# The count behind the last jump moved to the end of VectorE's work, and the transfers of a skipped loop given to GpSimd

## The chip, the cores and the metric

The kernel runs on one core of one Trainium2 chip. A core has five engines, each with an instruction stream of its own: TensorE (PE in the profile, its weight loads PEld), VectorE (DVE), ScalarE (ACT), GpSimd (POOL) and SyncE (SP), which here issues nearly all transfers. The engines wait for each other through semaphores. Sixteen DMA engines move the data. The metric is the time of one execution on the device in microseconds (us); lower is better.

## The reference

One transformer layer on 8,192 tokens (4 sequences of 2,048) of width 256, in float32: an attention inside chunks of 32 tokens without a softmax, a layer norm, a gated feed-forward part with integer weights, a second layer norm.

```python
Q, K, V = x @ W_q.T, x @ W_k.T, x @ W_v.T
decay = sigmoid(log_decay[0])
mask = where(diff >= 0, decay ** diff, 0)              # inside a chunk of 32
S = einsum('bncd,bnkd->bnck', Qc, Kc) * mask
O = einsum('bnck,bnkd->bncd', S, Vc)
a = sigmoid(x @ W_g.T) * O @ W_o.T + x
x = layernorm(x + a)
gate, up = x @ (w_gate / 127).T, x @ (w_up / 127).T    # 768 hidden features
x = layernorm(x + (silu(gate) * up) @ (w_down / 127).T)
```

The feed-forward weights are int32. `setup_inputs` draws them from -127 to 127.

## The kernel before, in words

The 8,192 tokens are taken in 16 blocks of 512 (`TB`). The Python loop `for b in range(NB - 2)` (line 938) is unrolled into one long program. Each pass runs the feed-forward part of block b while it prepares the attention of the blocks after it, so that TensorE always has products to do. A planner places the instructions of each engine; where the order matters it is pinned: `in_turn` (line 290) keeps an instruction behind all that were written before it for the same engine. Passes are alike and take 31.69 us each.

The feed-forward products split each float32 operand into a high and a low part, and this is exact enough only while every integer weight is at most 128 in magnitude (`EXACT`). So the kernel looks at the weights. `look_up` (line 264) takes the largest magnitude of each of nine weight pieces on VectorE, and `count_wide` (line 276), called in the pass b = 1 (line 978), counts how many of those maxima are above 128: a comparison, a product with ones on TensorE that adds over the partitions, a sum on VectorE into `count`, and a conversion to the integer `n_wide`.

After the last block's store comes the part for wide weights (lines 1174 to 1196). `nc.values_load` reads `n_wide` into a register of each of the five engines, and `tc.If(wide_any > 0)` makes each engine jump over the part if the count is 0, which it is with these inputs. The part itself holds nine transfers of weight pieces with a scaling of each, and a loop on the chip, `tc.For_i`, over all blocks; its body is `wide_block` (line 1128), which loads xT and x, computes the layer anew and stores. None of it is executed here, but it stands in the instruction streams, and what follows the jump has to bring the semaphores to what they would be had the part been run.

The transfers of the unrolled passes and of the skipped part are written with the same helpers: `load_xT` (116), `load_xn` (124) and `store` (857), which take a `start` that is `None` in the passes and the loop's register in the skipped part. All of them issue on SyncE's queue. The last block is finished group by group (lines 1102 to 1125): four groups of 128 tokens, of which ScalarE scales the first two and VectorE the last two (`by_vector`, line 874); each is stored by a transfer of its own of 128 KB (`store_groups`, line 1034, whose transfer is line 1037). What closes the program (semaphore waits and an exchange of all engines) is shown at line 1235.

Of the kernel before, what the change touches and what calls it, by code (L numbers as in the profile page):

```python
# [50 lines left out]
I32 = mybir.dt.int32  # L51
# [3 lines left out]
P = 128  # L55
# [16 lines left out]
def kernel(  # L72
# [15 lines left out]
    nc = tc.nc  # L88
# [7 lines left out]
    const = ctx.enter_context(tc.tile_pool(name="const", bufs=1))  # L96
# [12 lines left out]
    def bank(name):  # L109
        return psum.tile([P, TB], F32, tag="ps", name=name)  # L110


    def span(b, start):
        return slice(b * TB, (b + 1) * TB) if start is None else bass.ds(start, TB)

    def load_xT(b, start=None, pieces=1):
        xt = xin.tile([P, KD, TB], F32, tag="xT", name=f"xT_{b}")
        src = xT[:, span(b, start)].rearrange("(k p) t -> p k t", p=P)
        n = KD // pieces
        for k in range(0, KD, n):  # L120
            nc.sync.dma_start(xt[:, k : k + n, :], src[:, k : k + n, :])
        return xt

    def load_xn(b, start=None):
        xn = xin.tile([P, NG, D], F32, tag="x", name=f"x_{b}")
        nc.sync.dma_start(xn, x[span(b, start), :].rearrange("(g p) d -> p g d", p=P))
        return xn

    def load_w(eng, w, name):
# [146 lines left out]
    def count_wide():  # L276

        wide = const.tile([P, top.shape[1]], F32, tag="wide", name="wide")
        nc.vector.tensor_scalar(wide, top, EXACT, None, ALU.is_gt)
        ones = const.tile([P, 1], F32, tag="ones", name="ones")  # L280
        nc.vector.memset(ones, 1.0)
        pw = bank("pw")
        nc.tensor.matmul(pw[:1, : top.shape[1]], lhsT=ones, rhs=wide, start=True, stop=True)
        count = const.tile([1, 1], F32, tag="count", name="count")
        nc.vector.tensor_reduce(count, pw[:1, : top.shape[1]], mybir.AxisListType.X, ALU.add)
        n_wide = const.tile([1, 1], I32, tag="n_wide", name="n_wide")
        nc.vector.tensor_copy(n_wide, count)
        return n_wide

    def in_turn(ins):  # L290
        tc.keep_in_program_order(ins)
# [57 lines left out]
    def root_in_turn(mv, kind, name):  # L349
        return root(mv, name, kind[0], order=in_turn)  # L350
# [45 lines left out]
    def normalize(r, scale, shift, groups=range(NG)):  # L396
        for g in groups:
            in_turn(
                nc.scalar.activation(  # L399
                    r[:, g, :],  # L400
                    r[:, g, :],
                    AF.Identity,
                    bias=shift[:, g : g + 1],
                    scale=scale[:, g : g + 1],
                )
            )
# [319 lines left out]
    def move_h(b, h):  # L726

        sq = moved.tile([P, D // SQ, NG, SQ], F32, tag="sq", name=f"sq_{b}")
        for g in range(NG):
            in_turn(
                nc.vector.transpose(
                    sq[:, :, g, :], h[:, g, :].rearrange("p (j f) -> p j f", f=SQ)
                )
            )
        hT = moved.tile([P, KD, NQ, NG * SQ], F32, tag="hT", name=f"hT_{b}")
        for q in range(NQ):
            for j in range(NQ):  # L740
                nc.sync.dma_start(
                    hT[j * SQ : (j + 1) * SQ, :, q, :],
                    sq[q * SQ : (q + 1) * SQ, j::NQ, :, :].rearrange(
                        "p k g t -> p k (g t)"
                    ),
                )
        return hT
# [107 lines left out]
        return r, mv, made  # L855

    def store(b, r, start=None):
        nc.sync.dma_start(
            out[span(b, start), :].rearrange("(g p) d -> p g d", p=P), r
        )  # L860

# [76 lines left out]
    for b in range(NB - 2):  # L938
        n = b + 2
        m = b + 3  # L940
        more = m < NB
        xns[n] = load_xn(n)
        hT = hTs.pop(b)
        uT = [], []
        yT, v, sg = ahead
        steady = b > 0
        if b:
            normalize(hs[b + 1], *scales_h)
            moving = move_h(b + 1, hs[b + 1])
        ffn_up(b, hT, uT, range(0, 1))  # L950
        if b == 0:
            g_rest()
            x_sums = token_sums(xTs[m], f"x_{m}")
        ffn_up(b, hT, uT, range(1, 2))
        sT = attn_scores(n, yT)
        if m + 1 < NB:
            xTs[m + 1] = load_xT(m + 1)
        ffn_up(b, hT, uT, range(2, 3))
        if b == 0:

            normalize(hs[b + 1], *scales_h)
            moving = move_h(b + 1, hs[b + 1])
        if not more:
            normalize(r_before, *scales_out)
            store(b - 2, r_before)
        if more:
            v_next, v_rest = split_v(m, x_sums)
        multiply = ffn_up(b, hT, uT, range(3, 4), held=True)
        if more:
            v_rest()  # L970
        multiply()
        goT = attn_values(n, sT, v, sg)
        if scales_out is not None and more:
            normalize(r_before, *scales_out)
            store(b - 2, r_before)
        if b == 0:
            look_up(range(4, n_pieces))
        if b == 1:
            n_wide = count_wide()
        if more:  # L980
            go_sums = token_sums(goT, f"go_{n}")
            y_next, y_rest = split_y(m, x_sums)
        ffn_up(b, hT, uT, range(4, KH))
        r_before = r_out
        if more:
            y_rest()
            sg_next, g_rest = split_gate(m, x_sums)
            hs[n], out_rest = split_out(n, go_sums)
            g_rest()
            mv_h = out_rest()  # L990
            ahead = y_next, v_next, sg_next
            hTs[b + 1] = split_h(b + 1, moving)
            std_h = root_in_turn(mv_h, of_h, f"h_{b}")
            if b:
                mv_before, std_before = mv_out, root_in_turn(mv_out, of_out, f"out_{b}")
            back_to_sigmoids()
            if m + 1 < NB:

                x_sums = token_sums(xTs[m + 1], f"x_{m + 1}", in_turn)

            def between():
                return scale_and_shift(mv_h, std_h, of_h, f"h_{b}")

            r_out, mv_out, scales_h = ffn_down(b, uT, hs.pop(b), between)
            if b:
                scales_out = scale_and_shift(mv_before, std_before, of_out, f"out_{b}")
        else:

            hs[n] = attn_residual(n, goT)
            mv_h = moments(hs[n], f"a{n}", order=in_turn)  # L1010
            std_out = root_in_turn(mv_out, of_out, f"out_{b}")
            hTs[b + 1] = split_h(b + 1, moving)
            std_h = root_in_turn(mv_h, of_h, f"h_{b}")
            back_to_sigmoids()
            scales_out = scale_and_shift(mv_out, std_out, of_out, f"out_{b}")
            normalize(r_before, *scales_out)
            store(b - 1, r_before)

            inverse(std_h, slice(0, NG), HALF)
            for g in range(NG):  # L1020
                by_vector(hs[n], g, mv_h, std_h)
            r_out, mv_out, _ = ffn_down(b, uT, hs.pop(b), chunkwise=True)
            scales_out = iterated_scale_and_shift(mv_out, of_out, f"out_{b + 1}")
# [104 lines left out]
    def wide_block(start, weights):  # L1128
# [42 lines left out]
        project_back("w", (uT,), (rows,), residual, "fdn")  # L1171
        finish("w", r, start)

    wide_any = nc.values_load(
        n_wide, min_val=0, max_val=top.shape[1] * P, skip_runtime_bounds_check_because="a count"
    )
    with tc.If(wide_any > 0):

        homes = [
            pool.tile([P, KD, TB], F32, tag=tag, name=f"wide_{i}")  # L1180
            for i, (pool, tag) in enumerate(
                ((work, "hT_hi"), (work, "hT_hi"), (sums, "x_sums"), (sums, "g_sums"))
            )
        ]
        last_home = work.tile([P, TB], F32, tag="hT_lo", name="wide_last")
        room = [t[:, k, :] for t in homes for k in range(KD)] + [last_home]
        weights = []
        for w in (ffn_gT, ffn_uT, ffn_dT):
            weights.append([])
            for src in int_pieces(w):  # L1190
                t = room.pop(0).rearrange("p (k n) -> p k n", n=D)
                nc.sync.dma_start(t.bitcast(I32), src)
                nc.vector.tensor_scalar(t, t.bitcast(I32), SCALE, None, ALU.mult)
                weights[-1].append(t)
        with tc.For_i(0, NT, TB) as start:
            wide_block(start, weights)
# [42 lines left out]
```

## Time and profile before

| | us |
|---|---|
| median of 3 runs | 528.29 (527.94 to 528.46) |
| the profiled execution | 527.63 |
| its span, first to last instruction | 525.9 |
| outside its span | 1.73 |

| engine | busy us | share of the span |
|---|---|---|
| TensorE | 517.3 | 98% |
| VectorE | 389.8 | 74% |
| GpSimd | 343.2 | 65% |
| ScalarE | 322.3 | 61% |

The end of the program in this execution, in us from the span's start:

| what | when |
|---|---|
| TensorE reads the count, jumps | 517.2, 517.8 (the jump takes 2.245) |
| GpSimd reads the count | 519.2 |
| ScalarE reads the count | 520.2 |
| last scaling on VectorE | 520.80 to 521.21 |
| VectorE reads the count | 520.8 |
| last store issued on SyncE | 521.24, held 1.41 |
| SyncE reads the count, jumps | 522.7, 523.3 |
| SyncE's semaphore instructions behind the jump | 523.5 to 524.5 |
| closing waits and exchange | 524.5 to 525.8 |

Times come from the hardware profiler, which records one execution. An engine's name with a q behind it (SPq, PEldq) stands for the instructions of its sequencer: register loads, branches, semaphores, and the issuing of transfers; these are not counted as busy. A line number is one of the kernel before. DMA queues are numbered: 1 is SyncE's transfers, 8 and 14 bring instructions.

### The profile page before, as it was taken

The page shows a single profiled execution, that of the slowest core. Times are in us where ns is not written, and L with a number is a line of the kernel's source. Part 1 is how long each engine was busy: PE and PEld are TensorE (multiplying, and loading weights), DVE is VectorE, ACT ScalarE, POOL GpSimd, SP SyncE. Part 2 cuts the span into 40 slices and gives each one's busy share as a digit, 9 for nine tenths or more (in the row PEclk, how much of TensorE's full clock was granted, in tenths as well). Part 3 has the DMA queues.
Part 4 walks back from the last instruction along what each step waited for, and adds up shares of the span by engine and source line. Part 5 has one row for each costly group of instructions (what it writes and reads, how often), then busy time and mean ns, then how long its engine had stood idle before and what let it go on. Part 6 is the DMA issues. An engine that isn't in the chain of part 4 may idle for free.

```text
span 525.9 us, 10552 instructions
## 1 busy us (share of the span) xinstructions
PE 517.3 (98%) x3646; PEld 422.2 (80%) x3646; DVE 389.8 (74%) x964; ACT 322.3 (61%) x644; POOL 343.2 (65%) x476
## 2 busy tenths in 40 slices
PE   8999999999999999999999999999999999999994
PEld 5798887887978788887887978788887888878683
DVE  3878797686786867777677776867868677787865
ACT  2745565465656756666575655666666575667744
POOL 6535785766847668585776857668485675735653
PEclk9999999999999999999999999999999999999998
DMA  7721121213213131131312313141131312011201
GB/s 252 218 91 42 51 60 28 65 42 67 96 34 87 53 110 41 39 109 31 105 42 51 112 30 92 49 113 41 36 93 51 105 42 53 30 27 54 79 22 65
DMA packets 43256, 36.90 MB, mean 70 GB/s; under 512 B 4800, under 2 KB 39104, under 8 KB 43200
## 3 DMA queue, kind: packets, MB, share of 16 engines
q1 hardware_dynamic: 42240, 35.41, 23.2%
q8 instruction: 30, 0.49, 0.4%
q10 hardware_dynamic: 960, 0.79, 0.4%
q14 instruction: 26, 0.21, 0.2%
HBM read 20.45 MB, written 8.39 MB: 55 GB/s over the span
## 4 chain that ended last, share of the span: by engine, by line
PE 95%; DVE 2%; ACT 1%; POOL 1%; issue 0%; DVEq 0%; ACTq 0%
PE fg L776 16%; PE fu L776 16%; PE fdn L663 14%; PE p_v L462 9%; PE p_y L444 9%; PE p_g L444 9%; PE p_o L462 8%; PE po L637 5%; PE ps L616 3%; PE fdn L842 2%; PE pa L663 1%; PE pg L558 1%; PE pi L178 1%; PE pv L596 1%; PE py L575 1%; DVE st_f L311 0%
## 5 line engine op out<-in xcount | busy, mean ns | idle before, releaser
L801 POOL TENSOR_TENSOR u_lo<-u,u_hi 128x512 f16<-128x512 f32 (+1 forms) x98 | 123.0, 1257 | 111.0 <-ACT u_hi L800 109.6
L800 ACT CAST u_hi<-u 128x512 fp32r<-128x512 f32 (+1 forms) x98 | 59.7, 609 | 65.3 <-DVE u L798 64.9
L786 DVE SCALAR_TENSOR_TENSOR s<-fg,s 128x512 f32<-128x512 f32 (+1 forms) x98 | 65.9, 673 | 34.3 <-ACT s L784 34.1
L784 ACT ACTIVATE s<-fg 128x512 f32<-128x512 f32 (+1 forms) x98 | 56.9, 583 | 41.5 <-PE fg L776 41.4
L798 DVE TENSOR_TENSOR u<-fu,s 128x512 f32<-128x512 f32 (+1 forms) x98 | 66.4, 678 | 10.4 <-POOL u_lo L801 1.1
L776 PE MATMUL fg<-hT_hi,fg_hi 128*128 128x512 f32 (+1 forms) x196 | 74.0, 458 | 0.0
L776 PE MATMUL fu<-hT_hi,fu_hi 128*128 128x512 f32 (+1 forms) x196 | 60.5, 390 | 0.0
L776 PE MATMUL fg<-hT_lo,fg_lo 128*128 128x512 f16 (+1 forms) x196 | 58.0, 377 | 0.0
L776 PE MATMUL fu<-hT_lo,fu_lo 128*128 128x512 f16 (+1 forms) x196 | 57.4, 375 | 0.0
L663 PE MATMUL fdn<-fd_hi,u_hi 128*128 128x256 f32 x312 | 46.9, 292 | 0.0
L776 PEld LDWEIGHTS fu<-hT_hi,fu_hi 128*128 128x128 f32 x196 | 36.5, 188 | 8.5
L399 ACT ACTIVATE h<-h,shift_h,scale_h 128x256 f32<-128x256 f32 x52 | 27.0, 590 | 24.1 <-POOL shift_h L362 24.1
L776 PEld LDWEIGHTS fg<-hT_hi,fg_hi 128*128 128x128 f32 x196 | 34.6, 189 | 8.8
L663 PEld LDWEIGHTS fdn<-fd_hi,u_hi 128*128 128x128 f32 x312 | 39.8, 189 | 0.3
L663 PE MATMUL fdn<-fd_lo,u_lo 128*128 128x256 f16 x312 | 38.6, 273 | 0.0
L776 PEld LDWEIGHTS <-fu_lo 128*128 128x128 f16 x196 | 19.2, 98 | 22.2
L824 DVE SCALAR_TENSOR_TENSOR r<-fdn,h 128x512 f32<-128x512 f32 x30 | 20.7, 689 | 21.6 <-PE fdn L663 19.1
L759 POOL TENSOR_TENSOR hT_lo<-hT,hT_hi 128x512 f16<-128x512 f32 x28 | 35.3, 1280 | 1.2 <-ACT hT_hi L758 1.2
L776 PEld LDWEIGHTS <-fg_lo 128*128 128x128 f16 x196 | 15.3, 98 | 20.7 <-issue 12.9
L663 PEld LDWEIGHTS <-u_lo 128*128 128x128 f16 x312 | 28.4, 98 | 4.2
L462 PE MATMUL p_v<-v_sums,x_sums 128*128 128x128 f32 x240 | 31.7, 275 | 0.0
L637 PE MATMUL po<-sT,v 128*128 128x128 f32 x256 | 31.2, 275 | 0.0
(207 smaller groups left out, 1183.0 us busy)
## 6 DMA issues: line engine op xcount, KB each, us to landing
x<-in_x_dram SPq DMA_DIRECT2D x16, 512.0 KB, 3.5
xT<-in_xT_dram SPq DMA_DIRECT2D x15, 512.0 KB, 4.3
hT<-sq SPq DMA_DIRECT2D x224, 32.0 KB, 1.9
out_dram<-r SPq DMA_DIRECT2D x14, 512.0 KB, 5.0
fg_int<-in_ffn_gT_dram SPq DMA_DIRECT2D x3, 256.0 KB, 7.8
fu_int<-in_ffn_uT_dram SPq DMA_DIRECT2D x3, 256.0 KB, 7.0
fd_int<-in_ffn_dT_dram SPq DMA_DIRECT2D x3, 256.0 KB, 5.9
xT<-in_xT_dram SPq DMA_DIRECT2D x2, 256.0 KB, 4.2
```

What stands on the lines that cost most here:

```text
L399: nc.scalar.activation(r[:, g, :], r[:, g, :], AF.Identity, bias=shift[:, g : g + 1], scale=scale[:, g : g + 1],)
L444: nc.tensor.matmul(pb, lhsT=a[i - 1], rhs=b[i - 1], start=first, stop=True, skip_group_check=True,)
L462: nc.tensor.matmul(pb[:, g * P : (g + 1) * P], lhsT=b[i - 1][:, g * P : (g + 1) * P], rhs=a[i - 1], start=first and g == 0, stop=True, ski ...
L637: nc.tensor.matmul(po[:, cols], lhsT=v[:, g, dc * P : (dc + 1) * P], rhs=sT[:, cols], start=True, stop=True,)
L663: nc.tensor.matmul(pb[:, j * D : (j + 1) * D], lhsT=part[:, g * P : (g + 1) * P], rhs=w, start=(i == 0), stop=(i == len(terms) - 1),)
L759: nc.gpsimd.tensor_tensor(in_order[1], whole, in_order[0].bitcast(F32), ALU.subtract)
L776: nc.tensor.matmul(pb, lhsT=w[kind][:, dc, hc * P : (hc + 1) * P], rhs=hT[kind][:, dc, cols], start=(kind == kinds[0] and dc == 0), stop=( ...
L784: order(nc.scalar.activation(s, pg, AF.Sigmoid, scale=SCALE / H_UP))
L786: gated = nc.vector.scalar_tensor_tensor(s, pg, U_UP / H_UP**2, s, ALU.mult, ALU.mult)
L798: in_steady_turn(nc.vector.tensor_tensor(u, pu, s, ALU.mult))
L800: nc.scalar.copy(hi, u)
L801: nc.gpsimd.tensor_tensor(lo, u, hi.bitcast(F32), ALU.subtract)
```

## The change

Three things are changed.

The conversion of the count to an integer leaves `count_wide`, which now returns the float `count`. It is written just ahead of `nc.values_load`, pinned with `in_turn` behind everything that VectorE did before.

`load_xT`, `load_xn` and `store` choose their queue by `start`: SyncE in the unrolled passes as before, GpSimd in the loop of the skipped part.

The nine transfers of weight pieces in the skipped part are issued by GpSimd instead of SyncE. With this, nothing in the skipped part is issued by SyncE.

```diff
+    def queue(start):
+
+        return nc.sync if start is None else nc.gpsimd
+
     def load_xT(b, start=None, pieces=1):
...
-            nc.sync.dma_start(xt[:, k : k + n, :], src[:, k : k + n, :])
+            queue(start).dma_start(xt[:, k : k + n, :], src[:, k : k + n, :])
...
     def load_xn(b, start=None):
         xn = xin.tile([P, NG, D], F32, tag="x", name=f"x_{b}")
-        nc.sync.dma_start(xn, x[span(b, start), :].rearrange("(g p) d -> p g d", p=P))
+        src = x[span(b, start), :].rearrange("(g p) d -> p g d", p=P)
+        queue(start).dma_start(xn, src)
         return xn
...
         nc.vector.tensor_reduce(count, pw[:1, : top.shape[1]], mybir.AxisListType.X, ALU.add)
-        n_wide = const.tile([1, 1], I32, tag="n_wide", name="n_wide")
-        nc.vector.tensor_copy(n_wide, count)
-        return n_wide
+        return count
...
     def store(b, r, start=None):
-        nc.sync.dma_start(
+        queue(start).dma_start(
             out[span(b, start), :].rearrange("(g p) d -> p g d", p=P), r
         )
...
         if b == 1:
-            n_wide = count_wide()
+            count = count_wide()
...
+
+    n_wide = const.tile([1, 1], I32, tag="n_wide", name="n_wide")
+    in_turn(nc.vector.tensor_copy(n_wide, count))
     wide_any = nc.values_load(
         n_wide, min_val=0, max_val=top.shape[1] * P, skip_runtime_bounds_check_because="a count"
     )
...
-                nc.sync.dma_start(t.bitcast(I32), src)
+                nc.gpsimd.dma_start(t.bitcast(I32), src)
```

## The prediction

> **What bounds the kernel now.** I read the page from the top, then the chain, then the last stage engine by engine, because the changed lines act only at block 1 and after the last store.
>
> ```profile
> span 525.9 us, 10552 instructions
> PE 517.3 (98%) x3646; PEld 422.2 (80%) x3646; DVE 389.8 (74%) x964; ACT 322.3 (61%) x644; POOL 343.2 (65%) x476
> ...
> PE 95%; DVE 2%; ACT 1%; POOL 1%; issue 0%; DVEq 0%; ACTq 0%
> ```
>
> Busy time, and the chain by engine: TensorE carries 95% of the chain. Nothing that the change moves feeds a matmul, so the body should keep its length; what can change is the end. The last scalings on VectorE, from the timeline of 520.2 to 526 us, and below them the last store:
>
> ```profile
> 520.28 0.41 DVE L875 TENSOR_SCALAR r<-r,mv_f,rstd_f 128x256 f32<-128x256 f32 x1
> 520.80 0.41 DVE L875 TENSOR_SCALAR r<-r,mv_f,rstd_f 128x256 f32<-128x256 f32 x1
> ...
> 521.24 1.41 SPq L1037 DMA_DIRECT2D out_dram<-r  x1
> ```
>
> Compute ends at 521.21, and 4.6 us of the 525.85 us span remain. That tail is the subject. The instructions of the count's load (L1174), of the jump (L1177) and of the stores (L1037), duration min/median/max in ns, then first and last start:
>
> ```profile
> L1037 SPq DMA_DIRECT2D out_dram<-r x6: 333/358/1409, 511.1 to 521.2; - x6
> ...
> L1174 PEldq TENSOR_LOAD <-n_wide x1: 482/482/482, 517.2 to 517.2; - x1
> L1174 POOLq TENSOR_LOAD <-n_wide x1: 492/492/492, 519.2 to 519.2; - x1
> ...
> L1174 DVEq TENSOR_LOAD <-n_wide x1: 649/649/649, 520.8 to 520.8; - x1
> L1174 SPq TENSOR_LOAD <-n_wide x1: 516/516/516, 522.7 to 522.7; - x1
> ...
> L1177 SPq EVENT_SEMAPHORE  x8: 17/17/17, 523.5 to 524.5; - x8
> L1177 PEldq COMPARE_BRANCH  x1: 2245/2245/2245, 517.8 to 517.8; - x1
> ...
> L1177 DVEq COMPARE_BRANCH  x1: 72/72/72, 521.5 to 521.5; - x1
> ...
> L1177 SPq COMPARE_BRANCH  x1: 50/50/50, 523.3 to 523.3; - x1
> ...
> L1235 SPq EVENT_SEMAPHORE  x10: 17/28/28, 524.5 to 525.8; - x10
> ```
>
> Two things stand out. The last of SP's stores holds SP for 1409 ns where the median store takes 358 (the store issued at 519.2 took 345 ns and landed 1.7 us after its issue; the last lands 2.9 us after). And TensorE, which has its last matmuls before 518.9, jumps far ahead of everybody, at 517.8 to 520.1. What was on the DMA engines from 521.0 to 522.3:
>
> ```profile
> q1 hardware_dynamic: 271, 0.25, 56.2%
> q8 instruction: 1, 0.02, 5.8%
> ```
>
> One packet of queue 8, instructions, takes 5.8% of 16 engines over 1.3 us, so one DMA engine for 1.2 us. The window 518.8 to 521.0 has none, 517.3 to 518.8 has one. Queue 8 is TensorE's: 30 packets and 0.49 MB are 16 KB each, 256 instructions of 64 bytes, and 30 times 256 answers to TensorE's 7,292 weight loads and matmuls. So the packet at 521 is the fetch that follows TensorE's jump by 1 us, and it stands in the way of the last store. The same meeting is seen at 245.4: an SP issue of a hT piece takes 1954 ns (median 595) in a window with one queue 8 packet.
>
> The end is thus: last store landed at 524.2 (521.24 + 2.9), SP's remaining semaphore instructions until 525.03, the closing exchange of all engines until 525.85.
>
> **What the skill says.** The Trainium skill, "Runtime: NRT & Kernel Launch", section Instruction fetch mechanics: instructions come in 16 KiB blocks by a DMA queue of the sequencer, and a taken branch whose target isn't in the window forces a fetch before execution can go on. The trace agrees on the size (16 KB packets), and TensorE's jump of 2.245 us beside 0.05 on SP shows such a wait. "DMA: Bandwidth & Descriptors", section Issuing engines are not separate DMA queues: all issuers share 16 DMA engines; the collision above agrees. Its section SWDGE vs HWDGE vs iDMA: GpSimd's transfers have descriptors built in software; no run here shows one, and the skipped part executes none.
>
> **The change, part by part.** Start from the profiled execution: 527.63 us, 1.73 outside its span of 525.9; the median of the runs shown is 528.29, 0.66 more. I take differences from the profile and apply them to the median.
>
> 1. The conversion to integer leaves block 1: one CAST of 141 ns on VectorE at 95.9. VectorE is at 74% there and TensorE sets the pace: 0. If that cover were gone it would be −0.14. The order of the body could also be planned differently after it; I take 0, with a bound of a few us both ways in the range.
>
> 2. The same CAST now stands behind the last scaling: 521.21 + about 0.1 = 521.3. All five count loads wait for it. TensorE's moves from 517.2 to 521.35, GpSimd's from 519.2, ScalarE's from 520.2, VectorE's from 520.8. Behind each stands only its jump. VectorE's line is the longest: load 0.65, branch 0.07, gap 0.5, done at 522.7 (before: 522.2). SP's load does not wait longer: it comes after its last store in any case.
>
> 3. TensorE's jump: load to 521.85, branch from 522.0. The block asked for at 517.3 is there since 520.1, so I take 0.1 us for the branch instead of 2.245; done at 522.2. Its following fetch then starts 1 us later, at 523.1 instead of 521.05. At the issue of the last store (521.24) no fetch is running, so the issue takes 0.35 and the landing 1.7 us: 522.95 instead of 524.17. That is **−1.2 us**. Bounds: 0 if the fetch starts before 522.9 and still blocks one of the 16 engines; −1.2 if it misses it.
>
> 4. SP issues nothing inside the skipped part. Its eight L1177 semaphore instructions (523.5 to 524.5, about 0.067 apart) even out transfer semaphores that the part would have raised; I take them gone from SP. Four of them lie after the last landing: **−0.3**. SP reads the count at 521.65, jumps at 522.25, and waits for the last landing in the closing list.
>
> 5. GpSimd now has such semaphores for weights (9 pieces), xT, x and the store. As on SP, eight at 0.067: 0.5 us, from 522.0 to 522.6, beside the landing wait, so 0. SP's closing list grows from 8 pairs at 0.063 to perhaps 12: 0.25; but the last store's semaphore stands fourth in it, so eight pairs still follow, as now: 0, to +0.25. Software transfers may also add to GpSimd's closing clear, which is on the path (135 ns now): 0 to +0.3; I take **+0.1**.
>
> Sum: −1.2 − 0.3 + 0.1 = −1.4. Check by the end: landing 522.97, eight pairs to 523.5, closing exchange 0.8, end at 524.4 against 525.85. Profiled execution 527.63 − 1.4 = 526.2; median 528.29 − 1.4 = **526.9 us**. Own range from the bounds: 526.5 to 527.3.
>
> **Rivals.**
>
> *Part of the gain is lost (527.3 to 528.9).* TensorE's jump costs its 2.245 us anyway: from 522.0 to 524.25, its update is seen by SP at 524.4, end at 525.3, gain 0.5, time 527.8. Or its next fetch starts before the last store has landed on all 16 engines: the two stores before the last waited 1.5 us for one engine, and the gain shrinks to the 0.3 of step 4: 528.0. For it: TensorE's branch row is the only evidence on a jump of its length. Against: the fetch of 517.3 had the whole time to arrive.
>
> *Slower: a jump waits for its instructions in the open.* Before, the 2.2 us wait of TensorE's jump lay under the last matmuls and scalings. Now all jumps start after 521.9 and nothing covers them. GpSimd's skipped part grows by 12 transfers and their address work, so its target may lie outside what it has fetched. A full miss, estimated from TensorE's rows: 1.0 to start (jump over at 520.06, packet at 521.05), 1.2 for the packet, 1.3 until usable (packet of 517.4 over at 518.7, jump over at 520.06), 3.5 us. GpSimd's branch at 521.95 + 3.5 + 0.5 of semaphores + 0.1 is 526.05, plus 0.73 of closing is 526.8: +0.9, and 1.4 to 2 with a slower software semaphore update, so 529.2 to 530.3. It decides from a jump of 3.0 us on (end as before), and is measurable from 4.1 us in all. For it: GpSimd's part grows most. Against: its branch took 45 ns before. A body planned worse would end on this side too.
>
> *The change does nothing:* if the slow issue at 521.24 is not due to the fetch, only step 4 remains, 528.0. Against: the timing of 521.05 and the same pairing at 245.4.
>
> **How the numbers follow.** About 0.2% (1.06 us) is what a measurement of this kernel can tell from no change; the likeliest case, −1.4, lies just beyond it. Chances: likeliest case 0.50, of which 0.06 falls short of 1.06 us; part lost or nothing done 0.28, of which 0.03 passes it; slower 0.22. Hence faster 0.47, same 0.31, slower 0.22. For 8 in 10 I leave 0.08 below 526.4 and 0.12 above 529.3.
>
> **What would show it.** Step 1: the block rhythm of 31.69 us is unchanged up to compute's end at 521.2. Step 2: all five L1174 loads start after 521.3. Step 3: TensorE's COMPARE_BRANCH at about 100 ns, the last L1037 store at 350 ns with a landing of 1.7 us, the queue 8 packet after 522.9. Step 4: no SP semaphore instructions at L1177. Step 5: some on GpSimd, done before 523. Wrong if an engine's COMPARE_BRANCH after 521.9 takes over 2 us, if compute ends at another time, or if GpSimd's row at L1235 grows by more than 0.5 us.

## The result, and the profile after

The changed kernel takes 526.36 us in the median (525.92 to 527.06), the kernel before, run beside it, 528.13 us (527.48 to 528.46): a ratio of 0.9969 with a 95% interval of 0.9961 to 0.9978, or 1.77 us less. That is clear of the 0.2% that was called measurable. The profiled execution of the changed kernel took 526.4 us, its span 524.8.

The instructions of each engine stand in the same order as before; only the conversion has moved, and what lies in the skipped part. The page, its first lines and the chain by engine:

```profile
span 524.8 us, 10553 instructions
...
PE 517.6 (99%) x3646; PEld 422.3 (80%) x3646; DVE 389.8 (74%) x964; ACT 322.3 (61%) x644; POOL 343.0 (65%) x476
...
PE 96%; DVE 2%; ACT 1%; POOL 1%; issue 0%; DVEq 0%; ACTq 0%
```

Busy times are those of before within 0.3 us, so the gain is not in the body. The end of VectorE's work, from the timeline of VectorE, and the last store from that of SyncE:

```profile
520.77 0.41 DVE L878 TENSOR_SCALAR r<-r,mv_f,rstd_f 128x256 f32<-128x256 f32 x1
521.10 0.16 DVE L870 RECIPROCAL rstd_f<-rstd_f 128x1 f32<-128x1 f32 x1
521.29 0.41 DVE L878 TENSOR_SCALAR r<-r,mv_f,rstd_f 128x256 f32<-128x256 f32 x1
521.62 0.13 DVE L1179 CAST n_wide<-count 1x1 int32<-1x1 f32 x1
```

```profile
521.73 0.33 SPq L1040 DMA_DIRECT2D out_dram<-r  x1
```

The last scaling ends at 521.70, in the profile of before at 521.21. This 0.49 us is not of the change: comparing the starts of the matmuls one by one, the two executions differ by 0.49 us at the second product of the program, and stay within 0.05 us of that to the end. So the executions differ in how they begin (more on this in experiments 3 and 5), and I compare **the tail**, from the end of the last scaling to the end of the span: 4.64 us before, 3.11 now, 1.53 less. It is known from one execution of each kernel, the one profiled. Its parts, by line (stores L1040, count loads L1180, jump L1183, closing L1241; ns min/median/max, first and last start):

```profile
L1040 SPq DMA_DIRECT2D out_dram<-r x6: 332/345/372, 511.6 to 521.7; - x6
...
L1180 POOLq TENSOR_LOAD <-n_wide x1: 667/667/667, 521.8 to 521.8; - x1
...
L1180 PEldq TENSOR_LOAD <-n_wide x1: 669/669/669, 521.8 to 521.8; - x1
L1180 SPq TENSOR_LOAD <-n_wide x1: 523/523/523, 522.1 to 522.1; - x1
...
L1183 POOLq EVENT_SEMAPHORE  x4: 17/43/43, 522.7 to 523.0; - x4
...
L1183 PEldq COMPARE_BRANCH  x1: 445/445/445, 522.6 to 522.6; - x1
...
L1183 SPq COMPARE_BRANCH  x1: 50/50/50, 522.7 to 522.7; - x1
L1183 POOLq INC_SWDGE_SEM  x1: 177/177/177, 523.0 to 523.0; - x1
...
L1241 SPq EVENT_SEMAPHORE  x14: 17/28/28, 523.2 to 524.7; - x14
```

No store is held for longer than 372 ns; the longest was 1409. TensorE's jump takes 0.445 us instead of 2.245. SyncE has no semaphore instruction at the jump any more; GpSimd has five, the last of which (INC_SWDGE_SEM) raises eight semaphores. What ran on the DMA engines from 521.7 to 523.5, and, in the second fence, from 523.5 to the end:

```profile
q1 hardware_dynamic: 393, 0.35, 58.1%
```

```profile
q8 instruction: 1, 0.02, 4.7%
q14 instruction: 1, 0.01, 2.6%
```

The fetch behind TensorE's jump starts at 523.8; the last store landed at 523.46, 1.7 us after its issue. That queue 8 carries TensorE's instructions shows in the traces themselves: in all ten kernels measured here, its last packet starts 0.7 to 1.0 us after the end of TensorE's jump, wherever the jump lies.

### The profile page after: what moved, and what is told of

It is laid out like the page before. It is cut to its first block, busy times and chain, and to the rows that moved or that the text cites. A ratio compares the mean times of both kernels' runs of the same rounds, so it can differ in the third digit from the quotient of the medians.

```text
span 524.8 us, 10553 instructions
## 1 busy us (share of the span) xinstructions
PE 517.6 (99%) x3646; PEld 422.3 (80%) x3646; DVE 389.8 (74%) x964; ACT 322.3 (61%) x644; POOL 343.0 (65%) x476
## 4 chain that ended last, share of the span: by engine, by line
PE 96%; DVE 2%; ACT 1%; POOL 1%; issue 0%; DVEq 0%; ACTq 0%
PE fg L779 16%; PE fu L779 16%; PE fdn L666 14%; PE p_v L465 9%; PE p_y L447 9%; PE p_g L447 9%; PE p_o L465 8%; PE po L640 5%; PE ps L619 3%; PE fdn L845 2%; PE pa L666 1%; PE pg L561 1%; PE pi L183 1%; PE pv L599 1%; PE py L578 1%; DVE st_f L314 0%
## 5 line engine op out<-in xcount | busy, mean ns | idle before, releaser
L804 POOL TENSOR_TENSOR u_lo<-u,u_hi 128x512 f16<-128x512 f32 (+1 forms) x98 | 123.0, 1257 | 111.1 <-ACT u_hi L803 109.6
```

The costliest lines, as they stand in the source:

```text
L804: nc.gpsimd.tensor_tensor(lo, u, hi.bitcast(F32), ALU.subtract)
```

## The experiments

All these kernels compute the same with the same order of instructions in the body; three have extra small matmuls at the very start. Each is compared with the kernel before on its chip, and its tail is measured as above.

**1. The late count alone** (`e1_cast`): the change, with the queues left as before.

```diff
     def queue(start):
-        return nc.sync if start is None else nc.gpsimd
+        return nc.sync
...
-                nc.gpsimd.dma_start(t.bitcast(I32), src)
+                nc.sync.dma_start(t.bitcast(I32), src)
```

> Only the late count: the conversion stands behind the last scaling, the transfers of the skipped part stay on SyncE. The measure is the tail, from the end of VectorE's last scaling to the end of the span: 4.64 us before, 3.11 after. Theory A (the instruction fetch behind TensorE's jump stood in the way of the last store; the rest is SyncE's semaphore work): the last store is held 0.35 us and lands 1.7 us after its issue, but the eight semaphore instructions behind SyncE's jump stay, four of them after the landing; tail 3.45 us, time 1.2 us below before. Rival B (all of the gain is SyncE's semaphore work, the fetch is a bystander): no gain, 0. Rival C (late reading by itself shortens the end, all engines jumping at once): the whole gain, tail 3.1, -1.5 us or more.

Measured: 526.48 us against 528.02, ratio 0.9972 (0.996 to 0.9983), tail 3.42 us. The stores and SyncE's jump:

```profile
L1040 SPq DMA_DIRECT2D out_dram<-r x6: 332/345/372, 511.1 to 521.3; - x6
...
L1183 SPq EVENT_SEMAPHORE  x8: 17/17/17, 522.4 to 523.3; - x8
```

The hold on the last store is gone, the eight semaphore instructions are there. The tail is what theory A gave (3.45), 1.22 us less; rival B, which gave this kernel nothing, falls.

**2. The queues alone** (`e2_queue`): the conversion goes back into `count_wide`.

```diff
+        n_wide = const.tile([1, 1], I32, tag="n_wide", name="n_wide")
+        nc.vector.tensor_copy(n_wide, count)
+        return n_wide
-        return count
...
-    n_wide = const.tile([1, 1], I32, tag="n_wide", name="n_wide")
-    in_turn(nc.vector.tensor_copy(n_wide, count))
```

> Only the queues: GpSimd issues the skipped part's transfers, the count is converted in block 1 as before. Theory A: TensorE jumps at 517.8 as before, its fetch starts at 521.0, the last store is held 1.4 us and lands 2.9 us after its issue; SyncE has no semaphore instructions behind its jump and twelve pairs in the closing list, the last store's being the eighth, so four pairs follow the landing where twelve instructions did: tail 4.2 us, 0.4 us below before. Rival B: the whole gain, tail 3.1, -1.5. Rival C: 0.

Measured: 527.44 us against 528.02, ratio 0.9989 (0.9981 to 0.9997), tail 4.5 us. The stores of the last group and TensorE's jump:

```profile
L1042 SPq DMA_DIRECT2D out_dram<-r x5: 344/372/1257, 514.7 to 523.1; - x5
...
L1182 PEldq COMPARE_BRANCH  x1: 1905/1905/1905, 518.9 to 518.9; - x1
```

The fetch is back. In this execution it starts at 521.6 and meets the third of the last four stores, which is held 1257 ns, so that the fourth is issued 0.8 us late. A small gain is left: 0.58 us in the medians and 0.13 in the tail, where theory A gave 0.4. The profiled execution, at 528.34 us, was among the slowest of the 13.

**3. The fetch moved, nothing else** (`e3_pad`, then `e8_pad2`). TensorE's stream gets 16 matmuls of one column at the start, whose result nothing reads. They shift the places at which TensorE asks for its next block of instructions. In the first version one of the two large idle matmuls was dropped for them, in the second both are kept.

```diff
+    for _ in range(16):
+        tc.keep_in_program_order(
+            nc.tensor.matmul(
+                pi[:1, :1], lhsT=idle[:, :1], rhs=idle[:, :1], start=True, stop=True
+            )
+        )
```

> The kernel before with nothing moved but TensorE's instruction count: one of the two large idle matmuls at the start is replaced by 16 matmuls of one column (the idle result is read by nothing). That is some 60 instructions more, so TensorE crosses into its last block of instructions some 4 us earlier. Theory A: the fetch of 517.4 moves to about 513, TensorE's jump at 517.8 takes 0.1 to 0.5 us instead of 2.2, the fetch behind it comes at about 519 to 520, before the last store; that one is held 0.35 us and lands after 1.7 us: tail 3.45, -1.2 us apart from what the start gains or loses (up to 0.5). Rivals B and C: no change in the tail, 4.6.

Measured: 528.46 us against 528.02, ratio 1.0002 (0.9994 to 1.001), but a tail of 3.42 us. What the tail gained was lost elsewhere; in the profiled execution, which at 529.24 us was the slowest of the 13, it was lost at the start. The first eight products, before and in this kernel:

```profile
L558 PE MATMUL pg<-xT,wg x8: 592/592/866, 5.2 to 8.5; 128*128 128x512 f32 x8
```

```profile
L564 PE MATMUL pg<-xT,wg x8: 593/1061/1220, 5.3 to 11.3; 128*128 128x512 f32 x8
```

TensorE had been idle for 0.9 us before them and ran most of them at 1061 ns instead of 592; from the ninth product on all matmuls are 2.8 us later, and stay so. That the pause made them slow is not shown (see experiment 5). The repeat keeps TensorE busy up to its first product:

> As the padded kernel, but with both large idle matmuls kept and the 16 of one column behind them (0.8 us by the padded kernel's trace), so that TensorE does not start its first products slow. Nothing else differs from the kernel before. Theory A: the body as before, or up to 0.7 us later at the start; TensorE's fetch behind its jump before 520.5; last store held 0.35 us; tail 3.42 as in the padded kernel instead of 4.64; time 0.5 to 1.3 us below before. Rival (the place of the fetch is not what counts, only the late count): tail 4.6, time at or above before.

Measured: 527.01 us against 528.30, ratio 0.9988 (0.9976 to 1.0001; two of the ten executions lay near 529, the others between 526.7 and 527.2), tail 3.42 us. The interval just includes no change, so it is the tail that decides here. Stores and TensorE's jump, then the DMA queues from 519.3 to 520.4 and from 521.6 to 523.5:

```profile
L1043 SPq DMA_DIRECT2D out_dram<-r x4: 332/338/345, 519.7 to 521.7; - x4
...
L1183 SPq EVENT_SEMAPHORE  x8: 17/17/17, 522.8 to 523.7; - x8
L1183 PEldq COMPARE_BRANCH  x1: 358/358/358, 518.2 to 518.2; - x1
```

```profile
q8 instruction: 1, 0.02, 5.4%
```

```profile
q1 hardware_dynamic: 419, 0.38, 59.2%
q14 instruction: 1, 0.01, 1.9%
```

TensorE reads its count at 517.6, as early as ever, and its jump is short because its block has come in time. The fetch behind the jump runs before the last store and not across it, and the tail is the one of the late count, to the hundredth. So neither the late count nor the common jump shortens the end: the place of the fetch does. Rival C falls.

**4. The fetch put back on the last store** (`e4_cast_mid`): the changed kernel, with the conversion behind the residual of the last group instead of behind its scaling.

```diff
+        if g == NG - 1:
+            n_wide = const.tile([1, 1], I32, tag="n_wide", name="n_wide")
+            in_turn(nc.vector.tensor_copy(n_wide, count))
         mv = moments(r, f"f{last}_{g}", [g], order=in_turn)
...
-    n_wide = const.tile([1, 1], I32, tag="n_wide", name="n_wide")
-    in_turn(nc.vector.tensor_copy(n_wide, count))
```

> The changed kernel with the conversion placed four VectorE instructions and two scalings earlier, behind the residual of the last group, some 1.7 us before the end of the last scaling. Theory A: TensorE's jump and the fetch behind it move earlier by as much, the fetch starts about 0.5 us after the last store's issue and lies across its data; one of the 16 DMA engines ends late, landing 2.3 to 3 us after the issue instead of 1.7, tail 3.4 to 4.0 (after: 3.1), so +0.3 to +0.9 us against the changed kernel. Rival B: the tail of the changed kernel, 3.1. Rival C: the same or slightly less, 3.0 to 3.1, since the other engines jump earlier but SyncE does not.

Measured: 527.87 us against 528.02, ratio 0.9996 (0.9988 to 1.0005), tail 4.44 us. The last four stores with their landing, and the DMA queues from 522.06 to 523.5:

```profile
L1040 SPq DMA_DIRECT2D out_dram<-r x4: 332/338/344, 519.7 to 521.7; - x4
...
DMA to landing us min/median/max: 1.7/2.5/3.4
```

```profile
q1 hardware_dynamic: 266, 0.24, 49.9%
q8 instruction: 1, 0.02, 5.7%
```

No store is held at its issue, since the fetch starts at 522.1, after the last one. But it lies across their data. Of the last store's 16 parts, 15 have landed by 523.43, the last one comes at 524.93; the third of the four stores waits for its last part from 522.93 to 524.62. Nearly the whole gain is gone, from moving one conversion by six instructions. The direction was theory A's, the size was more than it gave.

**5. Both ways of moving the fetch are worth the same** (`e7_pad_queue`): the kernel of experiment 2, with GpSimd's queue and the early count, and the 16 small matmuls.

```diff
+    for _ in range(16):
+        tc.keep_in_program_order(
+            nc.tensor.matmul(
+                pi[:1, :1], lhsT=idle[:, :1], rhs=idle[:, :1], start=True, stop=True
+            )
+        )
```

> The queues as in the changed kernel, the count converted early in block 1 as before, and the 16 one-column matmuls at the start: the fetch is moved out of the last store's way without the late count. Theory A: tail 3.1 us, as in the changed kernel; time as the changed kernel's, +0 to +0.7 us for the start. Rival (late count needed): tail 4.2 to 4.6.

Measured: 526.59 us against 528.30, ratio 0.9976 (0.9962 to 0.9991), tail 3.0 us. The jump of TensorE and of SyncE with GpSimd's update, and SyncE's closing list:

```profile
L1188 PEldq COMPARE_BRANCH  x1: 358/358/358, 520.4 to 520.4; - x1
...
L1188 POOLq INC_SWDGE_SEM  x1: 177/177/177, 522.9 to 522.9; - x1
...
L1188 SPq COMPARE_BRANCH  x1: 50/50/50, 524.9 to 524.9; - x1
```

```profile
L1246 SPq EVENT_SEMAPHORE  x14: 17/28/28, 525.1 to 526.8; - x14
```

Without the late count the tail is even 0.11 us shorter than the changed kernel's. There SyncE's list begins 0.40 us after the end of SyncE's jump, here 0.14 us. The difference is GpSimd's update: in the changed kernel it comes only at 523.0, and SyncE's list waits for it first (more under step 5 below); here it came about 2 us before SyncE's jump ended.

The profiled execution began slowly, as in experiment 3; with 528.40 us it is one of two of the six executions that lay near 528.4, the other four lying near 526.5. The first eight products:

```profile
L569 PE MATMUL pg<-xT,wg x8: 592/812/1221, 6.3 to 11.1; 128*128 128x512 f32 x8
```

Here TensorE was not idle before them, and the first four still took more than 1020 ns.

**6. Another queue than GpSimd's** (`e5_act_queue`): the changed kernel with ScalarE's queue in its place.

```diff
-        return nc.sync if start is None else nc.gpsimd
+        return nc.sync if start is None else nc.scalar
...
-                nc.gpsimd.dma_start(t.bitcast(I32), src)
+                nc.scalar.dma_start(t.bitcast(I32), src)
```

> The changed kernel with the skipped part's transfers on ScalarE's queue instead of GpSimd's. ScalarE then has the eight semaphore instructions behind its jump (from 522.7, four behind the last landing), SyncE's closing list is eight pairs again instead of twelve. Theory A (SyncE's own run of instructions bounds the end of the changed kernel): the list is 0.25 shorter but its last pairs wait for ScalarE, 0.3 us behind the landing: tail 3.0 to 3.2, no difference in time. Rival (GpSimd's software semaphore update or its closing clear costs): tail 2.7 to 2.9.

Measured: 526.91 us against 528.30, ratio 0.9976 (0.9968 to 0.9985), tail 3.44 us, against both expectations. The jump's line shows why:

```profile
L1183 SPq EVENT_SEMAPHORE  x8: 17/17/17, 522.1 to 523.0; - x8
...
L1183 ACTq EVENT_SEMAPHORE  x1: 17/17/17, 521.9 to 521.9; - x1
```

SyncE issues nothing inside the skipped part of this kernel, and still carries the eight semaphore instructions. The tail is that of the late count alone (3.42). So it is not enough that SyncE issues nothing. Whether GpSimd's update costs time, the rival here, this kernel cannot tell; experiment 5 beside the changed kernel can.

**7. A jump in the open** (`e6_unrolled`): the changed kernel with the skipped loop written out.

```diff
-        with tc.For_i(0, NT, TB) as start:
+        for start in range(0, NT, TB):
             wide_block(start, weights)
```

> The changed kernel with the loop of the skipped part written out for all 16 blocks, so that the jump goes over some 800 more rows of TensorE's program, 640 of VectorE's and 260 of ScalarE's, past what has been fetched. Measures the rival of the prediction, a jump that waits for its instructions with nothing to cover it. If a full miss costs what TensorE's rows gave (3.5 us): TensorE's COMPARE_BRANCH or the instruction after it 3 to 3.5 us later, tail 5.2 to 5.8, time 2.1 to 2.7 us above the changed kernel, about 0.7 above before. If jumps cost little wherever they go: tail 3.1, no difference.

Measured: 529.07 us against 528.30, ratio 1.0018 (1.0012 to 1.0025), tail 5.75 us.

```profile
L1183 PEldq COMPARE_BRANCH  x1: 3746/3746/3746, 522.3 to 522.3; - x1
...
L1183 ACTq EVENT_SEMAPHORE  x1: 17/17/17, 525.2 to 525.2; - x1
L1183 DVEq EVENT_SEMAPHORE  x1: 21/21/21, 525.3 to 525.3; - x1
L1183 PEldq EVENT_SEMAPHORE  x1: 51/51/51, 526.1 to 526.1; - x1
```

With its target not fetched, TensorE's jump takes 3.75 us, and ScalarE and VectorE stand 3 us between their branch at 522.2 and the next instruction. SyncE's closing list needs all three; it waits first for VectorE and last for TensorE. This is the prediction's slower rival, at about the price that it was given (3.5 us; from the start of TensorE's branch to its next instruction it is 3.8). It needed only a longer skipped part, and it came on other engines than the prediction feared: GpSimd's jump took 45 ns here too.

## Why the prediction was right, and where not

The direction held, and so did the fetch as the main cause; the second, smaller cause held in size, but not in how it works. The forecast was 526.9 us, 1.4 us below before; the fall is 1.77 us in the medians and 1.53 us in the tail of the profiles. The time lies 0.14 us under the likeliest case's own range and 0.04 us under the lower end of the wide one.

- **Step 1, the conversion leaving block 1: 0.** Right; the body is the same instruction by instruction.
- **Step 2, the loads.** All five start behind 521.7; the prediction had them behind 521.3, and this profile runs 0.49 us later. Four at once take 0.655 to 0.675 us instead of 0.465 to 0.65; VectorE's line ended at 523.2, and its pair stands tenth in SyncE's list, so nothing waited for it.
- **Step 3, the fetch out of the last store's way: −1.2 us.** Right in cause and size: −1.22 in experiment 1, and as much in experiment 3 without a late count. TensorE's jump costs 0.445 us where 0.1 was taken; that only moves the fetch farther from the store.
- **Step 4, SyncE's semaphore instructions: −0.3 us.** The tail falls from 3.42 to 3.11 us between experiment 1 and the change, and from 3.42 to 3.0 between `e8_pad2` and experiment 5. The step's reason, as the prediction put it, "SP issues nothing inside the skipped part", is wrong: experiment 6 has that too and keeps all eight. Of the two queues tried, only GpSimd's takes them off SyncE. The semaphore numbers in the traces show why: GpSimd's transfers are counted on eight semaphores of their own, for which SyncE's closing list now waits as well, and those of SyncE's stores no longer have to be raised behind the jump. ScalarE's transfers share the ones of SyncE.
- **Step 5, GpSimd's own: +0.1 us.** The size is about right, the account is not. GpSimd has four semaphore instructions and the update of 177 ns, from 522.7 to 523.2; the prediction took them to be covered by the wait for the landing. But the order of SyncE's list was guessed wrong: GpSimd's eight semaphores stand first in it, not last, and the update is what raises them. The one that SyncE's list needs first is raised at 523.15, and SyncE, whose jump was over at 522.76, begins its list at 523.17. All twelve pairs then follow, and SyncE passes the last store's, the eighth, at 523.63, 0.17 us after the landing of 523.46. So the last landing no longer ends the tail, as the sum had it; the chain of GpSimd's load, jump and update and SyncE's twelve pairs does. From the last landing to the end of the list it is 0.48 us, in experiment 5, where the update came early, 0.32: this wait costs about 0.15 us. The closing clear takes 178 ns instead of 135, and the span ends 0.82 us after SyncE's last step before the exchange instead of 0.76: about +0.05.
- **Luck in the sum of the two.** The prediction let twelve instructions follow the last landing before and eight pairs after. Where GpSimd is early (experiment 5), it is four pairs, which saves more than step 4 gave; in the changed kernel the wait for GpSimd, which the sum had at nothing, takes part of that back. Two errors of opposite sign leave −0.31 where −0.2 was forecast.
- **The size.** The tail fell by 0.13 us more than the sum: step 3 gave 1.22 instead of 1.2, and steps 4 and 5 together 0.31 instead of 0.2. The other 0.24 us, between the tail and the medians, is within the spread of the runs (1.0 us before, 1.1 after). No cause for it was looked for; the medians also hold how each execution begins, which the tails leave out.
- **The rivals.** "Part of the gain is lost" did not come, but is one conversion away: experiment 4 is it, with 528.0 forecast for a fetch across the data and 527.87 measured. "A jump in the open" did not come because the skipped part stays short enough; experiment 7 puts its price at 3.75 us on TensorE and 3.0 us on ScalarE and VectorE. "The change does nothing" is excluded by experiment 3.

## What to carry to other kernels

When the last transfers of a kernel decide its end, look at what else is on the DMA engines at that moment: a fetch of instructions behind a jump takes one of the 16 engines for about 1 us (0.94 to 1.38 at the end of these kernels), and a transfer isn't done before its last sixteenth is. A jump over skipped work is best made early enough to lie under other work, or so late that its fetch comes after the last landing; between the two it is worst. And the time of a part that is never run still counts: how far the jump goes, and whose semaphores it has to bring up to date, were worth 2.6 and 0.3 to 0.4 us here. Reading the count at the very end can put another engine's part of the jump on the path, as GpSimd's here: experiment 5, with the early count, has the shorter tail, because GpSimd is done when SyncE needs it.

## What the runs showed of the hardware

A fetch of TensorE's instructions can delay other engines' transfers in two ways. One that is issued about when the fetch starts can be held on its own sequencer: 1409 ns in the kernel before and 1257 in experiment 2, instead of 345. In the trace of the kernel before, all 11 of SyncE's issues of more than 1.2 us after the first 10 us stand within 0.35 us of the start of such a fetch, and each is over 0.37 to 0.39 us after the fetch ends. Not every issue is held: five loads of inputs issued during a fetch took 0.37 us, and a store issued 0.26 to 0.30 us after the start of one in experiments 3 and 5 took 0.34 to 0.35. What decides this is open, and so is what the holds in the body cost. In the second way, a transfer already issued gets its last part late, by up to 1.7 us (the third of the last four stores in experiment 4).

A jump to instructions that have not been fetched took TensorE 3.75 us: 1.1 until the packet starts, 1.3 for the packet, 1.4 until the next instruction. To instructions already there it took 0.36 to 0.46 us.

Not expected at all was the start. In the profiles of experiment 3 (`e3_pad`) and experiment 5 the first products run at 1061 ns or more instead of 592 and the body is 2.8 and 2.7 us later, more than the change under study is worth. TensorE had been idle for 0.9 us before them in the one and not at all in the other, so a pause is not the whole cause. What goes with the slow products is the granted clock: the trace's record of full clock begins at 11.2 us in `e3_pad`, at 9.8 in experiment 5, at 5.6 in the kernel before and at 4.7 in `e8_pad2`, and of the eight products those that start after it take 592 to 600 ns (697 for the very first of `e8_pad2`). `e8_pad2` and experiment 5 begin with the same matmuls, so it differs between executions; why is open.
